# Neighbour lists split by upper and lower 64 rows in a four-layer graph attention kernel, and more row blocks worked on over all nodes

## The chip, the core and the metric

The kernel runs on one core of one Trainium2 chip, in one launch. The metric is device time in microseconds (us); lower is better. In the profile the engines are PE (TensorE matmuls), PEld (TensorE weight loads), DVE (VectorE), ACT (ScalarE), POOL (GpSimd) and SP (SyncE, which starts most DMAs).

## What is computed

There are 4096 nodes with 256 features and an adjacency matrix `adj` of 4096 x 4096 zeros and ones; a pair is an edge with a chance of 1/256, and the diagonal is set. Four attention layers follow one another, each with a residual and a layer norm: `x = layernorm(x + layer(x, adj))`.

```python
# layers 0 and 1: 4 heads of 64; layer 2: 2 heads of 128
e = leaky_relu(s[:, None] + d[None, :], 0.2)      # s, d: linear in x, per head
e = where(adj > 0, e, -inf)
out = softmax(e, axis=-1) @ h                      # h: a linear map of x, per head
# layer 3: one score, two softmaxes (of e and of -e), values of 256
new = concat([softmax(e) @ x, -softmax(-e) @ x]) @ fc_W;  out = elu(new)
```

## The kernel before

**Sparse row tiles.** The nodes are cut into 32 tiles of 128. For a row tile of 128 nodes, about 1600 of the 4096 nodes are neighbours of at least one of its rows. `Program.lists` (L293) finds them once, before and during layer 0. For each row tile it packs the neighbours into 13 list tiles of 128 places (`NG`), and adds the row tile itself as a 14th (`NP`). It does so with one-hots: `pack` (L427) compares, for each of the 31 other node tiles, the place of each node with a range of places (L440, on DVE), and multiplies the one-hot with the mask bytes on PE (L446). `windows` (L106) gives the range that a node tile's places can fall into, so that a one-hot is one to three list tiles wide. The result is `maskC`, the 128 x 14 x 128 mask bytes of a row tile, and `idx`, the node number of each place. `places` (L394) works the places out, per block of four row tiles. If a list overflows, a flag is set and a dense fallback runs after the packed program.

**Attention of one row tile** (`RowTile`, L606). It is done in two halves of seven list tiles. `load` (L632) starts the DMAs: the score row `S`, the mask, the row tile's own values, and an indirect gather on POOL for each of the other list tiles (L647), which brings 128 rows of `vals` (values and score terms of the layer, `ROW[n]` floats) into a buffer `G`. First-half gathers read only the first 17 node tiles (`MIX`), so that they can start before all of the layer's values are there. `half` (L651) then makes the weights `w`, 128 list nodes by 128 rows per list tile: three of the four heads in layers 0 and 1 with one ACT exponential per list tile (L712), the fourth with DVE products (L704, L708); then one DVE operation per pair of heads clamps and masks seven list tiles of both (L681). In layers 0 and 1 the matmul (L724) has the values as weights (65 columns) and moves the 128 columns of `w`, so the result is transposed, and `copy` and `back` (L744, L751) turn it again. In layers 2 and 3 the matmul (L727) has `w` as weights (128 columns) and moves the values (129 or 257 columns). The arithmetic is fp32; one such matmul is two instructions, each with its own weight load.

**Row blocks over all nodes.** `WHOLE` (L94) lists blocks of four row tiles that use no lists: blocks 3, 7 and 6 in layer 2, and 7 in layer 3. `whole_rows` (L982) goes over all 32 node tiles, with exponentials (L1016, L1019 to L1023), masks (L1017, L1024) and matmuls (L1027). It is a generator, and `whole` (L804) advances it between the halves of the sparse row tiles, so that its work is spread over the layer.

**Order.** `part` (L812) goes over the row tiles, half by half. In layers 0 and 1 `half_alone` (L827) also projects finished row tiles for the next layer (`Projection`, L531); in layers 2 and 3 `half_with_whole` (L859) does, and advances the whole blocks. `close` (L919) passes from one layer to the next. `norm` (L1049) gathers row tiles in groups (`GROUPS`, L76) for the inverse square root. Each engine's final order is set by a scheduler from priorities in program order.

The `G` buffers: `g0` has 16 slots of two list tiles (one in layer 3), `g1` 14.

Of the kernel before, what the change touches and what calls it, by code (L numbers as in the profile page):

```python
# [50 lines left out]
P = 128  # L51
N = 4096
F = 256
# [17 lines left out]
NG = 13  # L71
NP = NG + 1
CAP = NG * P
HALF = NP // 2

GROUPS = (((24, 4),), ((28, 2),), ((16, 2), (17, 1), (20, 2), (24, 1), (31, 2)), ((28, 1), (31, 4)))  # L76
LEAD = 10
MIX = 17
FRONT = 6
NODES = tuple(MIX * P if t < FRONT else N for t in range(NG))  # L80
MC = P + 4
# [6 lines left out]

LOGS = (3, 3, 2, 1)
# [3 lines left out]
KEXP = 10.0  # L93

# [4 lines left out]
WHOLE = ((), (), (3, 7, 6), (7,))  # L99
# [6 lines left out]
def windows():  # L106

    share = 1.0 - (1.0 - 1.0 / 256.0) ** P
    mean, sd = P * share, (P * share * (1.0 - share)) ** 0.5
    dev = 4.5  # L110
    out = {}
    for m in range(NT):
        for j in range(NT):
            if j == m:
                continue
            if j < MIX:
                n = sum(q != m for q in range(j))
                lo = mean * n - dev * sd * n ** 0.5
                hi = mean * (n + 1) + dev * sd * (n + 1) ** 0.5
            else:  # L120
                n = sum(q != m for q in range(j, NT))
                lo = CAP - mean * n - dev * sd * n ** 0.5
                hi = CAP - mean * (n - 1) + dev * sd * (n - 1) ** 0.5
            a = max(0, int(lo // P))
            b = min(NG - 1, int((hi - 1) // P))
            out[m, j] = (a, b - a + 1)
    return out
# [3 lines left out]
assert all(a >= FRONT for (m, j), (a, _) in WINDOW.items() if j >= MIX)  # L131
WMAX = max(n for _, n in WINDOW.values()) * P
# [7 lines left out]
def kernel(ctx: ExitStack, tc: tile.TileContext, ins: dict, out: bass.AP):  # L140
# [11 lines left out]
        "shift2": const.tile([P, 1], F32, name="shift2"),  # L152
        "shift3": const.tile([4, 4], F32, name="shift3"),
        "zero": const.tile([4, 4], F32, name="zero"),
        "maskC": dram.tile([NT, P, NP, MC], U8, name="maskC"),
# [8 lines left out]
    nc.vector.memset(shared["shift2"], -2.0 * KEXP)  # L164

# [28 lines left out]
class Program:  # L194


    def __init__(self, tc, ctx, ins, out, shared):
# [5 lines left out]
        self.g0 = self.pool("g0", 16)  # L203
# [6 lines left out]
        self.masks = None  # L210
# [82 lines left out]
    def lists(self, ctx):  # L293
# [21 lines left out]
        for k, sh in enumerate((8, 4, 0)):  # L315
# [21 lines left out]
        nc.gpsimd.affine_select(out=bt[:, :, :MIX], in_=bt[:, :, :MIX], pattern=[[NT, BT], [1, MIX]],  # L337
                                compare_op=ALU.is_gt, fill=0.0, base=0, channel_multiplier=-1)
        nc.vector.tensor_scalar(bt[:, :, MIX:], bt[:, :, MIX:], -1.0, None, op0=ALU.mult)

        nc.gpsimd.affine_select(out=bt[:, :, MIX:], in_=bt[:, :, MIX:], pattern=[[-NT, BT], [-1, NT - MIX]],
                                compare_op=ALU.is_ge, fill=0.0, base=-MIX, channel_multiplier=1)


        lo = cst.tile([P, NT, NT], F16, name="lo")
        wid = cst.tile([P, NT, NT], F16, name="wid")
        nc.gpsimd.memset(lo, 0.0)
        nc.gpsimd.memset(wid, 0.0)
        for j in range(NT):
            m = 0  # L350
            while m < NT:
                if m == j:
                    m += 1
                    continue
                e = m
                while e < NT and e != j and WINDOW[e, j] == WINDOW[m, j]:
                    e += 1
                a, n = WINDOW[m, j]
                nc.gpsimd.memset(lo[:, m:e, j], a * P - 1.0 - (CAP if j >= MIX else 0))
                nc.gpsimd.memset(wid[:, m:e, j], float(n * P))  # L360
                m = e
        limit = cst.tile([P, NP], F32, name="limit")
        nc.vector.memset(limit[:, :FRONT], float(MIX * P - 1))
        nc.vector.memset(limit[:, FRONT:], float(N - 1))
        total = cst.tile([P, NT], F32, name="total")
        bad = cst.tile([P, BT, NT], F32, name="bad")
        nc.vector.memset(bad, 0.0)

        class Block:
            def __init__(self, blk):  # L370
                self.blk = blk
                self.mk = mkp.tile([P, NT, BT, MC], U8, name="mk")
                self.red = wk.tile([P, BT, NT], F32, name="red")

            def prepare(self, part):
# [5 lines left out]
                for q in range(q0, q1, 2):  # L381
# [4 lines left out]
                nc.vector.tensor_copy(mkw[:, q0:q1, :, P // 4:],  # L386
                                      digw[:, q0:q1].rearrange("p (j t o) -> p j t o", t=1, o=1)
                                      .to_broadcast([P, JG, BT, 1]))
                nc.vector.tensor_reduce(self.red[:, :, q0:q1].rearrange("p t j -> p j t"),
                                        mkw[:, q0:q1, :, :P // 4], AX.X, ALU.max)  # L390
# [3 lines left out]
            def places(self):  # L394
                blk = self.blk
                if any(blk in w for w in WHOLE):
                    nc.sync.dma_start(out=shared["maskW"][blk], in_=self.mk)
                hit = wk.tile([P, BT, NT], BF16, name="hit")
                nc.vector.tensor_scalar(hit, self.red, 0.0, None, op0=ALU.is_gt)
                flat = hit.rearrange("p t j -> p (t j)")  # L400
                nc.vector.memset(flat[:, blk * BT:blk * BT + (BT - 1) * (NT + 1) + 1:NT + 1], 0.0)
                pt = prog.bank(prog.pthree)
                nc.tensor.matmul(pt[:, :P], flat, ones, start=True, stop=True)
                totals = wk.tile([P, P], BF16, name="totals")
                nc.scalar.copy(totals, pt[:, :P])
                pq = prog.bank(prog.pthree)
                nc.tensor.matmul(pq[:, :P], tri, flat, start=True, stop=False, skip_group_check=True)
                nc.tensor.matmul(pq[:, :P], totals, bt.rearrange("p t j -> p (t j)"), start=False, stop=False,
                                 skip_group_check=True)
                nc.tensor.matmul(pq[:, P:P + BT], totals, tot, start=False, stop=True, skip_group_check=True)  # L410
                ms = slice(blk * BT, (blk + 1) * BT)
                self.place = wk.tile([P, BT, NT], F32, name="place")
                here = self.place
                nc.vector.tensor_tensor(here, pq[:, :P].rearrange("p (t j) -> p t j", t=BT), lo[:, ms, :],
                                        op=ALU.subtract)
                nc.vector.tensor_tensor(here, here, hit, op=ALU.mult)
                nc.vector.tensor_copy(total[:, ms], pq[:, P:P + BT])

                for col in (wid[:, ms, :], None):
                    off = wk.tile([P, BT, NT], F32, name="off")  # L420
                    if col is None:
                        nc.vector.tensor_scalar(off, here, 0.0, None, op0=ALU.is_lt)
                    else:
                        nc.vector.tensor_tensor(off, here, col, op=ALU.is_gt)
                    nc.vector.tensor_tensor(bad, bad, off, op=ALU.max)
# [180 lines left out]
class RowTile:  # L606
# [144 lines left out]
    def back(self):  # L751
        L = self.layer
        if L.n >= 2:
            return
# [835 lines left out]
```

## Time and profile before

| | us |
|---|---|
| median of three runs | 2251.94 (2251.93 to 2260.22) |
| span of the profiled execution | 2249.3 |
| PE busy | 2014.0 (90%), 15689 instructions |
| DVE busy | 1786.6 (79%), 5060 |
| ACT busy | 1737.9 (77%), 4989 |
| POOL busy | 1494.4 (66%), 1597 |

The span runs from the first to the last instruction of one execution. The costliest groups of instructions are below (line, engine, operation, out<-in, partitions x elements, count; busy us, mean ns of one; idle time of the engine just before them and what ended it):

```profile
L647 POOL DMA_INDIRECT G<-vals,idx x1456 | 1480.7, 1017 | 715.7 <-issue 221.1
L712 ACT ACTIVATE w<-S,G 128x128 f32<-128x128 f32 x3248 | 1001.6, 390 | 140.6 <-DMA G<-vals,idx 101.6
L724 PE MATMUL bank<-w,G 128*65 128x128 f32 x7168 | 837.8, 276 | 59.7 <-DVE w L681 59.3
L681 DVE SCALAR_TENSOR_TENSOR w<-w,bank 128x1792 f32<-128x1792 f32 x256 | 514.6, 2013 | 13.4 <-ACT w L712 11.2
L727 PE MATMUL bank<-G,w 128*128 128x257 f32 (+1 forms) x2660 | 490.8, 342 | 25.7 <-ACT z L1102 13.6
L446 PE MATMUL bank<-mk,oh 128*128 128x132 fp8e4 x2336 | 192.1, 226 | 13.8 <-ACT cm L453 7.0
```

Busy time counts overlapping instructions of an engine once, so a group's busy time divided by its count is nearer to the pace than the mean of one.

### The profile page before, as it was taken

The numbers are of one execution on the slowest core, as the hardware profiler recorded it, in microseconds if no ns is written. First come the engines' busy times: TensorE is split into PE (matmuls) and PEld (weight loads), VectorE is DVE, ScalarE is ACT, GpSimd is POOL, SyncE is SP. The second block draws the span as 40 slices with busy tenths as digits, with TensorE's granted clock in tenths as the row PEclk, the third lists the DMA queues.
The fourth block names the chain that finished last, engine by engine and source line by source line (L and its number), as shares of the span: only waits on it lengthen the run. The fifth ranks groups of instructions, "written<-read, shape, count | busy, mean of one in ns | idle before, by whom it ended". The sixth has DMA issues, their size and how long they took to land. (4 is left out here: it accounts for less than half of the span.)

```text
span 2249.3 us, 49137 instructions
## 1 busy us (share of the span) xinstructions
PE 2014.0 (90%) x15689; PEld 1834.3 (82%) x15689; DVE 1786.6 (79%) x5060; ACT 1737.9 (77%) x4989; POOL 1494.4 (66%) x1597
## 2 busy tenths in 40 slices
PE   4878889989999969988899898989999999999995
PEld 2658788878899859988888798989998888788784
DVE  2889899999999959987988886887876566566566
ACT  4778988988789859987888776987876677667664
POOL 2107655656677777777777777777773477777773
PEclk7999999999999989999999999999999999999998
DMA  8879877777566665666665666777777688888884
GB/s 284 258 245 360 272 219 250 254 247 228 146 170 191 174 202 168 182 175 175 173 185 162 172 167 171 226 209 223 223 227 225 200 282 280 249 284 270 262 248 130
DMA packets 250319, 492.99 MB, mean 219 GB/s; under 512 B 44385, under 2 KB 156610, under 8 KB 249666
## 3 DMA queue, kind: packets, MB, share of 16 engines
q0 software_dynamic: 81536, 245.30, 38.3%
q1 hardware_dynamic: 163906, 240.26, 33.3%
q10 hardware_dynamic: 4608, 4.20, 0.5%
q8 instruction: 126, 2.06, 0.4%
q14 instruction: 143, 1.17, 0.2%
HBM read 437.05 MB, written 52.54 MB: 218 GB/s over the span
## 5 line engine op out<-in xcount | busy, mean ns | idle before, releaser
L647 POOL DMA_INDIRECT G<-vals,idx x1456 | 1480.7, 1017 | 715.7 <-issue 221.1
L712 ACT ACTIVATE w<-S,G 128x128 f32<-128x128 f32 x3248 | 1001.6, 390 | 140.6 <-DMA G<-vals,idx 101.6
L724 PE MATMUL bank<-w,G 128*65 128x128 f32 x7168 | 837.8, 276 | 59.7 <-DVE w L681 59.3
L724 PEld LDWEIGHTS bank<-w,G 128*65 128x65 f32 x7168 | 798.7, 140 | 69.9 <-DVE w L681 68.4
L681 DVE SCALAR_TENSOR_TENSOR w<-w,bank 128x1792 f32<-128x1792 f32 x256 | 514.6, 2013 | 13.4 <-ACT w L712 11.2
L727 PE MATMUL bank<-G,w 128*128 128x257 f32 (+1 forms) x2660 | 490.8, 342 | 25.7 <-ACT z L1102 13.6
L727 PEld LDWEIGHTS bank<-G,w 128*128 128x128 f32 x2660 | 431.9, 195 | 73.2 <-ACT z L1102 16.4
L1027 PE MATMUL bank<-vw,pw 128*128 128x129 f32 (+1 forms) x2048 | 298.5, 301 | 3.7 <-issue 2.3
L1027 PEld LDWEIGHTS bank<-vw,pw 128*128 128x128 f32 x2048 | 273.6, 191 | 20.1 <-issue 2.8
L690 ACT ACTIVATE w<-S,G 128x128 f32<-128x128 f32 x385 | 137.8, 393 | 136.8 <-DMA G<-vals,idx 90.0
L440 DVE TENSOR_SCALAR oh<-iota,place 128x256 bf16<-128x256 f16 (+2 forms) x992 | 221.8, 298 | 9.4 <-PE bank L446 9.1
L704 DVE TENSOR_TENSOR w<-S,G 128x256 f32<-128x256 f32 x384 | 151.9, 416 | 69.9 <-DMA G<-vals,idx 66.5
L446 PE MATMUL bank<-mk,oh 128*128 128x132 fp8e4 x2336 | 192.1, 226 | 13.8 <-ACT cm L453 7.0
L557 PE MATMUL bank<-wext,xT 128*128 128x268 f32 (+3 forms) x640 | 176.9, 409 | 16.9 <-ACT xT L548 14.1
L446 PEld LDWEIGHTS <-oh 128*128 128x128 bf16 x2336 | 146.9, 99 | 50.4 <-DVE oh L440 12.7
L385 ACT ACTIVATE mk<-raw 128x1024 uint8<-128x1024 int32 x128 | 130.5, 1051 | 28.0 <-DMA raw<-in_adjB_dram 27.7
L557 PEld LDWEIGHTS bank<-wext,xT 128*128 128x128 f32 x640 | 117.2, 200 | 36.0 <-ACT xT L548 16.9
L1017 DVE SCALAR_TENSOR_TENSOR pw<-pw,mw 128x512 f32<-128x512 f32 x192 | 127.6, 689 | 18.2 <-ACT pw L1016 17.5
L1016 ACT ACTIVATE pw<-Sw,d 128x512 f32<-128x512 f32 x192 | 133.2, 711 | 7.5 <-PE bank L1027 7.0
L714 DVE SCALAR_TENSOR_TENSOR w<-w,mk 128x896 f32<-128x896 f32 x80 | 86.6, 1086 | 41.1 <-ACT w L712 37.9
L1024 DVE TENSOR_TENSOR pw<-pw,mw 128x512 f32<-128x512 f32 x64 | 43.6, 691 | 85.4 <-ACT pw L1023 48.0
L692 DVE TENSOR_TENSOR w<-w,mk 128x896 f32<-128x896 f32 x55 | 60.0, 1091 | 59.5 <-ACT w L691 58.2
(140 smaller groups left out, 1563.3 us busy)
## 6 DMA issues: line engine op xcount, KB each, us to landing
raw<-in_adjB_dram SPq DMA_DIRECT2D x128, 512.0 KB
mk<-maskC SPq DMA_DIRECT2D x112, 231.0 KB
G<-vals,idx POOLq DMA_INDIRECT x1456
S<-edge SPq DMA_DIRECT2D x64, 256.0 KB
vw<-vals SPq DMA_DIRECT2D x96, 129.0 KB
xp<-y SPq DMA_DIRECT2D x96, 128.0 KB
y<-xp SPq DMA_DIRECT2D x96, 128.0 KB
mw<-maskW SPq DMA_DIRECT2D x20, 528.0 KB
```

What stands on the lines that cost most here:

```text
L440: nc.vector.tensor_scalar(oh[:, :n * P], iota[:, :n * P], self.place[:, it, j:j + 1], None, op0=ALU.is_equal)
L446: nc.tensor.matmul(accs[b][:, s * MC:(s + 1) * MC], oh[:, (k - a) * P:(k - a + 1) * P], mk[:, j, it, :].bitcast(FP8), start=touches[b][0] ...
L557: nc.tensor.matmul(pp[:, :c1 - c0], self.xT[:, k, :], wext[:, k, c0:c1], start=(k == 0), stop=(k == KT - 1 and brow is None))
L647: nc.gpsimd.indirect_dma_start(out=self.place(pos), out_offset=None, in_=sh["v"][n][:NODES[t], :], in_offset=bass.IndirectOffsetOnAxis(ap= ...
L681: nc.vector.scalar_tensor_tensor(pair, pair, LEAST, mh2, op0=ALU.max, op1=ALU.mult)
L690: nc.scalar.activation(w[0][:, k, :], S[:, 0, :], AF.Relu, bias=d(k, 0))
L704: nc.vector.tensor_tensor(w[h][:, k:k + 2, :], S[:, h:h + 1, :].to_broadcast([P, 2, P]), dd[:, :, V + T + h:V + T + h + 1].to_broadcast([P ...
L712: nc.scalar.activation(w[h][:, k, :], S[:, h, :], AF.Exp, bias=d(k, h))
L724: nc.tensor.matmul(accs[0][:Wd, h * P:(h + 1) * P], v, w[h][:, k, :], **how)
L727: nc.tensor.matmul(a, w[h][:, k, :], v, **how)
L1016: nc.scalar.activation(p, S[:, h], AF.Exp, bias=d)
L1027: nc.tensor.matmul(accs[it][:, c:c + Wd], p[:, it, :], v[:, c:c + Wd], start=(j == 0 and h == heads[0]), stop=(j == NT - 1), skip_group_ch ...
```

## The change

1. **Lists.** A neighbour of a row tile is put into one of three classes: it is adjacent to rows 0 to 63 only, to rows 64 to 127 only, or to both. Five list tiles hold the first class, five the second, three the third and what overflows from the first two. There are 13 gathers per row tile as before, but an upper and a lower tile share one 128 x 128 unit of weights, 64 columns each: 9 units per row tile (five pairs, three whole, the row tile's own) instead of 14. `maskC` is 9 units wide. The first half has the row tile itself and three pairs (four units), the second two pairs and three whole list tiles (five).
2. **Weights and matmuls.** A pair's exponentials are done in two instructions of 64 columns, with each list tile's own bias. In all layers `w` is now the matmul's weights and the values are moved. A list tile of a pair has 64 weight columns and writes output rows 0 to 63 or 64 to 127, so a pair is two matmuls. `copy` and `back` are gone. Within a half, pairs and whole units are kept together.
3. **Whole blocks.** `WHOLE` has blocks 7 and 6 in layer 1 and 7 and 6 in layer 3. A new generator, `whole_heads`, does layer 1's: the weights are a product of a row term and a node term, so one DVE operation per head and node tile makes, clamps and masks them, without ACT. Two heads are worked on together, one with the weights `p` loaded, the other with the values loaded and turned afterwards.
4. **Buffers and limits.** `g0` and `g1` have four slots, each of seven list tiles (four in layer 3). First-half gathers read the first 23 node tiles. The groups of `norm` are fitted to the new order.

The core of the diff (`places` is longer by the arithmetic of the classes):

```diff
-NG = 13
-NP = NG + 1
-HALF = NP // 2
+NPAIR = 5
+NMIX = 3
+NPACK = NPAIR + NMIX
+NU = NPACK + 1
+NP = 2 * NPAIR + NMIX
+HALF = 7
+FIRST = 3
+UNITS = (1 + FIRST, NPACK - FIRST)
+FULL = ((0,), tuple(range(NPAIR - FIRST, NPACK - FIRST)))
+PAIRS = (tuple(range(1, 1 + FIRST)), tuple(range(NPAIR - FIRST)))
-MIX = 17
+MIX = 23
+TWOS = ((3, 0), (2, 1))
-WHOLE = ((), (), (3, 7, 6), (7,))
+WHOLE = ((), (7, 6), (3, 7, 6), (7, 6))
-        self.g0 = self.pool("g0", 16)
+        self.g0 = self.pool("g0", 4)
-        self.g1 = self.pool("g1", 14)
+        self.g1 = self.pool("g1", 4)
...
             def pack(self, it):
...
+                def parts(j):
+                    a, n, e, x = WINDOW[j]
+                    return list(range(a, a + n)) + list(range(NPAIR + e, NPAIR + e + x))
...
-                    nc.vector.tensor_scalar(oh[:, :n * P], iota[:, :n * P], self.place[:, it, j:j + 1], None,
-                                            op0=ALU.is_equal)
-                    for k in range(a, a + n):
+                    nc.vector.tensor_scalar(oh[:, :len(ks) * P], iota[:, :len(ks) * P], self.place[:, it, j:j + 1],
+                                            None, op0=ALU.is_equal)
+                    for i, k in enumerate(ks):
...
             for h in range(A):
-                for k in range(HALF):
-                    nc.scalar.activation(w[h][:, k, :], S[:, h, :], AF.Exp, bias=d(k, h))
+                for u in range(U):
+                    for rows, g in parts[u]:
+                        nc.scalar.activation(w[h][:, u, rows], S[:, h, rows], AF.Exp, bias=d(g, h))
...
-                if n < 2:
-                    nc.tensor.matmul(accs[0][:Wd, h * P:(h + 1) * P], v, w[h][:, k, :], **how)
-                else:
-                    a = accs[h][:, :Wd] if n == 3 else accs[0][:, h * Wd:(h + 1) * Wd]
-                    nc.tensor.matmul(a, w[h][:, k, :], v, **how)
+        for t, heads in enumerate(turns):
+            for us in (FULL[half], PAIRS[half])[::-1 if t == 1 and (half == 1 or n < 3) else 1]:
+                for h in heads:
+                    for u in us:
+                        for rows, g in parts[u]:
+                            a = accs[h][rows, :Wd] if n == 3 else accs[0][rows, h * Wd:(h + 1) * Wd]
+                            nc.tensor.matmul(a, w[h][:, u, rows], g[:, h * Wd:(h + 1) * Wd],
+                                             start=half == 0 and u == 0 and (n == 3 or h == turns[0][0]),
+                                             stop=half == 1, skip_group_check=True)
...
+    def whole_heads(self):
...
+        c = prog.bk.tile([P, NT, T], F32, name="cw")
+        nc.scalar.activation(c, sh["d"][n], AF.Exp, bias=sh["shift1"])
...
+                    for h in (up, flat):
+                        p[h] = prog.dp.tile([P, BT, P], F32, name="pw")
+                        nc.vector.scalar_tensor_tensor(p[h], S[:, h], c[:, j, h:h + 1], mj, op0=ALU.max, op1=ALU.mult)
+                    how = dict(stop=j == NT - 1, skip_group_check=True)
+                    for it in range(BT):
+                        nc.tensor.matmul(bu[:, it * Wd:(it + 1) * Wd], p[up][:, it, :],
+                                         v[:, up * Wd:(up + 1) * Wd], start=j == 0 and it == 0, **how)
+                        nc.tensor.matmul(bf[:Wd, it * P:(it + 1) * P], v[:, flat * Wd:(flat + 1) * Wd],
+                                         p[flat][:, it, :], start=j == 0 and it == 0, **how)
+                    yield
```

## The prediction

> **What bounds the kernel now.** I read the profile stage by stage, because the page's shares (PE 90%, DVE 79%, ACT 77%, POOL 66%) average over stages with different limits. The stage borders come from first and last starts: the lists' one-hots (L440) run from 56.8 to 641.0 us, ten lists before layer 0's first attention and 22 beside it; layer 0 ends at 812, layer 1 at 1346, layer 2 at 1742, and the last matmul of layer 3 starts at 2226. The view of windows over these borders (columns: window; busy us and instructions of PE, PEld, DVE, ACT, POOL; granted clock; DMA share; GB/s):
>
> ```profile
> 57.00:165.00 108.00, 90.54 (x893) 69.82 (x893) 94.57 (x423) 80.69 (x205) 7.69 (x8) 0.94 0.80 251
> 165.00:644.00 479.00, 428.80 (x4282) 392.87 (x4283) 461.96 (x1374) 414.50 (x1232) 305.96 (x301) 0.98 0.75 244
> 644.00:812.00 168.00, 156.42 (x1351) 149.89 (x1350) 154.35 (x378) 146.61 (x509) 126.44 (x131) 0.99 0.65 181
> 812.00:1346.00 534.00, 474.81 (x3995) 443.89 (x3993) 445.47 (x1011) 437.33 (x1470) 406.44 (x419) 0.97 0.63 175
> 1346.00:1742.00 396.00, 371.52 (x2977) 357.57 (x2977) 303.94 (x855) 308.25 (x839) 284.10 (x259) 0.98 0.75 215
> 1742.00:2226.00 484.00, 461.76 (x2083) 399.01 (x2083) 299.60 (x909) 321.93 (x682) 350.10 (x342) 0.98 0.82 255
> ```
>
> POOL looks slack until its timeline is read: a gather is busy 0.95 us, and 0.30 us pass before the next although nothing is waited for.
>
> ```profile
> 924.65 0.94 POOL L647 DMA_INDIRECT G<-vals,idx  x1 [0.30 <-issue]
> 925.90 0.95 POOL L647 DMA_INDIRECT G<-vals,idx  x1 [0.30 <-PE bank L724]
> 927.15 0.94 POOL L647 DMA_INDIRECT G<-vals,idx  x1 [0.30 <-issue]
> ```
>
> So POOL is full at one gather per 1.255 us, 16.3 us per row tile of 13. Layer 1's 419 gathers need 526 of its 534 us: POOL bounds it. The tail of layer 0 too (131, 164 of 168). In 165 to 644 it is DVE, 462 of 479 us. Layer 2 has two near limits (PE 372; POOL 284 busy and 259 x 0.30 = 362, of 396). Layer 3 is bound by PE (462 of 484), with POOL behind it (342 x 1.255 = 429). The chain of waits, in layer 3, is nothing but matmuls (start, us, what):
>
> ```profile
> 1846.88 1.73 PE bank L1027 x8
> 1848.61 6.07 PE bank L727 x28
> 1854.68 1.73 PE bank L1027 x8
> ```
>
> **PE rows to price with.** An fp32 matmul is two instructions, each with its weight load.
>
> ```profile
> 820.19 0.95 PE L278 MATMUL bank<-ablk,nat 128*128 128x2 f32 x8
> 821.24 1.05 PE L278 MATMUL bank<-ablk,nat 128*128 128x2 f32 x8
> 905.48 6.28 PE L724 MATMUL bank<-w,G 128*65 128x128 f32 x56
> 911.60 0.27 PE L589 MATMUL bank<-ident,row 128*2 128x128 f32 x1
> 911.71 0.38 PE L543 MATMUL bank<-ident,y 128*128 128x128 f32 x2
> 1848.45 6.23 PE L727 MATMUL bank<-G,w 128*128 128x257 f32 x28
> ```
>
> 257 moving columns cost 0.217 each (6.07/28). 128 columns under a 65-column load: (6.28-0.28)/55 = 0.109. L278 moves only 2 columns, so its (1.05-0.25)/7 = 0.114 is the price of loading 128 weight columns; I use 0.112. So an instruction costs the larger of 0.00085 us per moving column and 0.00088 us per weight column.
>
> **The change, part by part.**
>
> *Lists, DVE.* One-hots stay 992, mean width 262 columns to 488 (341 of 640, 248 of 512, 279 of 384, 124 of 256). By the groups 256 cost 0.291 and 384 cost 0.316, 0.02 per 100, so 640 is 0.383: mean 0.299 to 0.345, +1.42 us per list. The placing grows from nine operations per block (2.1 us) to 13 of 256 elements (0.416 each, the row of L704), 9 of 128 (0.286, L414) and some small ones: 10.3 us, +8.2 per block, +2.05 per list. Small ones +0.25. Together +3.7 per list. PE: 2336 to 3782 packing matmuls at 0.07 (57 in 4.13 us at L446), +3.2 per list.
>
> *Sparse attention, layers 0 and 1, DVE.* A row tile has 9 units instead of 14 tiles of weights. Mask: 4 x 2.013 becomes 2 x 1.22 and 2 x 1.48 (1.035 ns per element, from 896 = 1.086 and 1792 = 2.013), -2.65. Products: 6 x 0.416 + 2 x 0.295 becomes 2 x 0.551 + 0.416 + 0.295, -1.27. Mask copy -0.17. In all -4.1, to 7.8 us per tile (5.4 + 1.8 + 0.6).
>
> *PE there.* Out go 112 instructions of 0.109 (12.2 us) and the transposes back (4 in 0.46). In come 80 with 64 weight and 65 moving columns and 32 with 128 and 65. The 32 are bound by their load, 0.112. For the 80 no row exists: at most 0.109 (L724), at least 0.025 (four tiny ones of L287 in 0.24, less their latency); by columns 0.058, which I take. 80 x 0.058 + 32 x 0.112 = 8.2, -4.3 us per tile. ACT: 42 exponentials (0.29 apart) become 30 of 64 columns and 12 of 128, about -1.6 us, never first.
>
> *Layer 0's sum.* From 57 to 165 (ten lists, no attention, DVE at 88%, PE at 84%): DVE +3.7 x 10 = +37, of which slack takes some 12: **+25 us**. From 165 to 644: 22 x (3.7-4.1) = **-9**. Its tail is POOL's, 13 gathers as before: 0. Range -5 to +60, the end being both engines' growth in a row.
>
> *Layer 1.* 8 of 32 tiles leave POOL: 24 x 16.3 = 392 us against 526. But they go to PE and DVE. PE: sparse 24 x 8.2 = 197; dense 2048 instructions, half with 128 weight and 65 moving columns, half the reverse, alternating in pairs so that a long load lies under a long matmul: two long, one short and one long in four, (3 x 0.112 + 0.058)/4 = 0.098, 200 us; the rest as before, 475 - 3584 x 0.109 - 8 = 76; 96 switches between whole-array and half-array weights. Bounds for a switch: nothing (L589, with 2 weight columns, lies between L724 and L543 without a gap) and 0.09 (L560, one weight row, is 0.98 behind four L557 that take 0.88). I take 0.09: 9 us. Sum 482. DVE: 445 - 32 x 4.1 - 8 x 7.8 + 256 x 0.67 (L1017) + 6 = 428. PE is the new bound; at the 97% that DVE reached in layer 0, 497 of 534: **-37**. Range -75 (POOL and PE even at 455) to 0.
>
> *Layer 2.* Its tiles need 20 x 56 instructions of 0.112 now, then 20 x (40 x 0.058 + 16 x 0.112), -43 on PE if two halves run beside each other in the array, nothing if not. POOL stays at 362: **-12**, range -25 to +5.
>
> *Layer 3.* POOL: 24 tiles instead of 28. Only two tiles' first halves now fit in the slots ahead, not four, so about 303 gathers fall into the stage, 380 us. PE: dense 1024 x 0.217 = 222 instead of 111; a sparse tile has 16 whole instructions (3.5 us) and 40 with 64 weight columns and 257 moving ones. These cost 0.217 if alone in the array, 0.109 if the upper and the lower half stream side by side. No row shows two at once. I take side by side, because the halves write different output partitions, hold different weights and are emitted alternately: 24 x (3.5+4.4) = 188; sum 188 + 222 + 11 (rest) + 11 (120 switches) = 432, and 22 us of gaps as before, 454 of 484: **-30**. The other end is worked out below.
>
> *Costed at nothing.* A slot now holds seven gathers (four in layer 3), so a gather waits for the last matmul of a whole half, and all later gathers queue behind it on POOL. Four slots per pool leave POOL three halves ahead, 3 x 8.2 = 24 us, and a half needs some 15 us (6.5 of exponentials, 2 x 1.4 of masks, 4 of matmuls). Should that cover go, POOL idles up to 4 us per half, 190 us over layer 1. First halves now read 23 node tiles, not 17; at both layer ends these are projected before the last tile, and the second half waits for all 32 as before. SP issues 192 more loads of some 130 KB, POOL 156 fewer gathers of as much; DMA is busy 63% in layer 1 and 82% in layer 3, so they hide.
>
> [...] With a full latency of a matmul (0.27) at each of some 500 switches the sum would lose another 90 us.
>
> Sum: 25 - 9 - 37 - 12 - 30 = -63. The profiled execution spans 2249.3 us; 2186 after. The median of the runs shown, 2251.94, lies 2.6 above the span: **2189 us**.
>
> **Rivals.**
> 1. *The halves don't run side by side (slower).* Place: layer 3's PE. Price: 40 x 0.108 x 24 = 104 us more, 536 + 22 = 558 of 484, +74; layer 2 gains 0; layers 0 and 1 keep theirs, since 65 moving columns are short. 25 - 9 - 37 + 0 + 74 = +53: 2305. It decides once a half costs over 0.17 instead of 0.109. For it: PE already bounds this stage and gets a whole dense block more. Against: distinct output rows.
> 2. *The lists and DVE take the gain back.* Phase 57 to 165 pays +50, from 165 on the longer placing chain (PE, ACT, PE, then 22 dependent DVE operations) stalls the full DVE, +15, and layer 1, with DVE at 428 and PE at 482 feeding each other, reaches 88%: 548, +14. 50 + 15 + 14 - 12 - 30 = +37 at its worst, and +5 in the middle: 2257.
> 3. *POOL remains the only bound.* Switches cost nothing, PE needs 470 in layer 1 and runs without gaps, layer 3 follows POOL with 380 + 40: 15 - 9 - 60 - 20 - 55 = -129: 2123.
>
> **Chances.** The sum as worked 0.50 (2150 to 2235), rival 1 0.21, rival 2 0.15, rival 3 0.14. Faster or slower than 0.5% (11 us, about what a measurement can tell): the sum 0.48 faster; rival 3 all; rival 2 0.05 faster, 0.06 same, 0.04 slower; rival 1 slower. Faster 0.67, same 0.08, slower 0.25. The range takes in most of rivals 1 and 3: 2115 to 2305; the likeliest case alone is 2150 to 2235.
>
> **What would show it.** Side by side: pairs of the 64x257 row 0.11 apart on average, not 0.217. Layer 1: about 500 us, PE over 95% busy, POOL with waits. Lists: the last one-hot later than 641 by 10 to 30 us. Layer 0's tail still one gather per 1.255 us. Layer 3 near 455 us. I am wrong if layer 3 grows, or if a switch leaves gaps of 0.2 us on PE.

## The result, and the profile after

The changed kernel takes 2319.51 us (median of four runs, 2312.40 to 2335.76) where before takes 2256.08 beside it (2251.93 to 2260.27): ratio 1.0294, 95% interval 1.0265 to 1.0323. It is **slower**; the forecast was 2189. The profiled execution took 2323.15 us, its span is 2321.4.

The stages, by the prediction's borders (first one-hot, L504; end of the tenth and of the last list; statistics of a layer's last row tile; start of the last matmul):

| stage | before | after | forecast | measured |
|---|---|---|---|---|
| to the first one-hot | 57 | 70 | with the next | +13 |
| ten lists | 108 | 153 | +25 | +45 |
| 22 lists beside attention | 479 | 531 | -9 | +52 |
| tail of layer 0 | 168 | 173 | 0 | +5 |
| layer 1 | 534 | 513 | -37 | -21 |
| layer 2 | 396 | 395 | -12 | -1 |
| layer 3 | 484 | 468 | -30 | -16 |
| end | 23 | 18 | | -5 |
| sum | 2249 | 2321 | -63 | +72 |

The same windows in after's trace (columns as in the prediction):

```profile
70.00:223.00 153.00, 120.19 (x1408) 102.40 (x1409) 125.49 (x495) 81.01 (x194) 16.71 (x12) 0.87 0.67 216
223.00:754.00 531.00, 438.18 (x5130) 401.65 (x5126) 455.26 (x1453) 338.67 (x1115) 285.10 (x293) 0.75 0.63 193
754.00:927.00 173.00, 136.17 (x1336) 117.81 (x1337) 118.42 (x360) 128.32 (x509) 126.29 (x132) 0.74 0.66 186
927.00:1440.00 513.00, 469.98 (x5015) 424.55 (x5011) 433.56 (x1045) 292.51 (x1112) 303.60 (x293) 0.92 0.65 187
1440.00:1835.00 395.00, 357.69 (x3014) 327.10 (x3015) 284.43 (x868) 294.03 (x852) 272.50 (x260) 0.96 0.71 204
1835.00:2303.00 468.00, 447.33 (x2386) 328.39 (x2384) 278.82 (x890) 328.22 (x744) 319.08 (x312) 0.98 0.84 268
```

The second row is the surprise. DVE is busy 455 us, where the forecast had 462 - 9 = 453, yet the stage is 531 long. DVE fills 86% of it (before 96%), PE 83%, and PE's granted clock is 0.75 where it was 0.98. Layers 2 and 3 kept their clock (0.96 and 0.98, before 0.98 in both). The page's slices show it over the whole span: it is 6 to 8 tenths up to the 17th slice (986 us), and 9 after that but for one slice within layer 1 and the ends of layers.

```profile
PE   4867787888788868699899989797999899989996
PEld 2757787777677757699788986787989767757774
DVE  2978988888888767699897986477787746565665
ACT  4554757676655867546545665587788568766873
POOL 0012654455446677777746630777777177767773
PEclk7878777777778786799989997899999999999998
```

POOL's pace is unchanged, 1.25 us from one gather to the next (tail of layer 0, timeline):

```profile
821.95 0.95 POOL L714 DMA_INDIRECT G<-vals,idx  x1 [0.30 <-PE bank L819]
823.20 0.95 POOL L714 DMA_INDIRECT G<-vals,idx  x1 [0.30 <-issue]
824.45 0.95 POOL L714 DMA_INDIRECT G<-vals,idx  x1 [0.30 <-issue]
```

**How the clock falls.** Six neighbouring windows of 3.4 us in after, within the 22 lists (columns as above; the granted clock stands behind the five engines):

```profile
303.30:306.70 3.40, 3.33 (x57) 3.15 (x54) 3.40 (x11) 1.11 (x2) 2.49 (x4) 1.00 0.98 385
306.70:310.10 3.40, 1.01 (x9) 1.01 (x10) 3.39 (x11) 3.40 (x13) 2.49 (x4) 1.00 1.01 318
310.10:313.50 3.40, 2.52 (x27) 2.00 (x28) 3.05 (x9) 3.40 (x15) 0.96 (x1) 0.51 1.00 375
313.50:316.90 3.40, 3.40 (x28) 3.28 (x27) 2.79 (x9) 3.40 (x15) 0.00 (x0) 0.50 0.58 216
316.90:320.30 3.40, 3.40 (x38) 3.16 (x38) 0.58 (x2) 1.81 (x7) 2.25 (x3) 0.50 0.16 40
320.30:323.70 3.40, 3.40 (x63) 3.19 (x61) 3.36 (x9) 0.00 (x0) 2.48 (x4) 0.99 0.47 126
```

In the second window PE works 1.01 of 3.4 us, because it waits 2.46 us for the masks of the next half (L763). The following three windows run at half clock: 27 to 38 matmuls instead of 57 to 63. PE is full from the second of them on, and in the fifth window DVE does 0.58 us of work, since its one-hot buffers wait for PE. So each engine waits for the other in turn. Counted over the whole span from the trace's clock records, the clock was halved 52 times in after and 23 times in before.

Half of the 531 us, 268, run at half clock. DVE is busy in 93% of the time at full clock and in 79% of that at half clock, and of the 55 us that it waits for one-hot buffers here, 44 fall at half clock. The same wait in before, in its stage of 479 us (us, times, longest):

```profile
DVE oh L440 <- PE bank L446: 4.3, 1, 4.3
```

### The profile page after: what moved, and what is told of

It reads as the page before. It is cut to its first block, busy times and chain, and to the rows that moved or that the text cites. A ratio compares the mean times of both kernels' runs of the same rounds, so it can differ in the third digit from the quotient of the medians.

```text
span 2321.4 us, 54044 instructions
## 1 busy us (share of the span) xinstructions
PE 2002.1 (86%) x18383; PEld 1723.4 (74%) x18383; DVE 1730.0 (75%) x5248; ACT 1499.3 (65%) x4596; POOL 1328.9 (57%) x1374
## 5 line engine op out<-in xcount | busy, mean ns | idle before, releaser
L714 POOL DMA_INDIRECT G<-vals,idx x1300 | 1323.3, 1018 | 955.4 <-issue 380.7
L819 PE MATMUL bank<-G,w 128*64 128x65 f32 (+5 forms) x8708 | 844.7, 299 | 119.4 <-DVE w L763 100.2
L819 PEld LDWEIGHTS bank<-G,w 128*64 128x64 f32 (+1 forms) x8708 | 694.2, 180 | 272.0 <-DVE w L763 114.7
L805 ACT ACTIVATE w<-S,G 128x64 f32<-128x64 f32 (+1 forms) x2912 | 784.3, 352 | 129.9 <-DMA G<-vals,idx 107.6
L1102 PE MATMUL bank<-vw,pw 128*128 128x129 f32 (+1 forms) x2560 | 422.8, 323 | 18.0 <-issue 6.7
L1102 PEld LDWEIGHTS bank<-vw,pw 128*128 128x128 f32 x2560 | 377.4, 196 | 58.8 <-issue 18.1
L763 DVE SCALAR_TENSOR_TENSOR w<-w,bank 128x1024 f32<-128x1024 f32 (+1 forms) x224 | 301.3, 1346 | 34.8 <-ACT w L805 34.1
L504 DVE TENSOR_SCALAR oh<-iota,place 128x640 bf16<-128x640 f16 (+3 forms) x992 | 284.3, 351 | 57.2 <-PE bank L510 56.7
L510 PE MATMUL bank<-mk,oh 128*128 128x136 fp8e4 x3782 | 263.2, 232 | 6.3 <-ACT cm L516 4.0
L510 PEld LDWEIGHTS <-oh 128*128 128x128 bf16 x3782 | 248.3, 103 | 13.5 <-DVE oh L504 4.5
L1162 DVE SCALAR_TENSOR_TENSOR pw<-Sw,cw,mw 128x512 f32<-128x512 f32 x256 | 183.6, 740 | 1.4 <-issue 1.2
L1165 PE MATMUL bank<-vw,pw 128*128 128x65 f32 x1024 | 151.7, 267 | 17.8 <-DVE pw L1162 17.8
L1167 PE MATMUL bank<-pw,vw 128*65 128x128 f32 x1024 | 163.3, 277 | 0.0
L773 ACT ACTIVATE w<-S,G 128x64 f32<-128x64 f32 (+1 forms) x329 | 104.6, 352 | 85.4 <-DMA G<-vals,idx 47.7
L1165 PEld LDWEIGHTS bank<-vw,pw 128*128 128x128 f32 x1024 | 139.9, 195 | 20.9 <-issue 19.6
```

The costliest lines, as they stand in the source:

```text
L504: nc.vector.tensor_scalar(oh[:, :len(ks) * P], iota[:, :len(ks) * P], self.place[:, it, j:j + 1], None, op0=ALU.is_equal)
L510: nc.tensor.matmul(accs[b][:, s * MC:(s + 1) * MC], oh[:, i * P:(i + 1) * P], mk[:, j, it, :].bitcast(FP8), start=touches[b][0] == (j, k), ...
L714: nc.gpsimd.indirect_dma_start(out=self.place(half, k), out_offset=None, in_=sh["v"][n][:N if half else MIX * P, :], in_offset=bass.Indire ...
L763: nc.vector.scalar_tensor_tensor(pair, pair, LEAST, mh2, op0=ALU.max, op1=ALU.mult)
L805: nc.scalar.activation(w[h][:, u, rows], S[:, h, rows], AF.Exp, bias=d(g, h))
L819: nc.tensor.matmul(a, w[h][:, u, rows], g[:, h * Wd:(h + 1) * Wd], start=half == 0 and u == 0 and (n == 3 or h == turns[0][0]), stop=half ...
```

## The experiments

Two kinds of chips were met. On those of the result above and of e1 to e4, before takes 2254 to 2256 us. On three others before takes 2752 to 2798 and after 2868 to 2920, ratio 1.0385 to 1.0474. There the stages ahead of the attention are as long as ever (after's ten lists take 153 to 155 us), the later ones longer. Kernels are compared on their own kind of chip. In the table, layers end with the statistics of their last tile, also layer 3; rounded us:

| kernel | before there | total | ratio, 95% interval | first one-hot | ten lists | 22 lists | layer 1 | layer 2 | layer 3 |
|---|---|---|---|---|---|---|---|---|---|
| before | | 2256.1 | | 57 | 109 | 478 | 534 | 396 | 495 |
| after | 2256.1 | 2319.5 | 1.0294 (1.0265-1.0323) | 70 | 154 | 531 | 514 | 394 | 479 |
| e1 | 2253.8 | 2335.1 | 1.0349 (1.0290-1.0407) | 70 | 153 | 520 | 527 | 383 | 505 |
| e2 | 2253.8 | 2300.5 | 1.0199 (1.0153-1.0244) | 69 | 154 | 509 | 524 | 382 | 480 |
| e3 | 2253.8 | 2284.3 | 1.0161 (1.0107-1.0214) | 69 | 180 | 471 | 514 | 392 | 479 |
| e4 | 2253.8 | 2296.1 | 1.0185 (1.0144-1.0226) | 71 | 150 | 507 | 515 | 396 | 478 |
| e5 | 2797.6 | 2891.1 | 1.0328 (1.0282-1.0373) | 69 | 153 | 724 | 705 | 506 | 521 |
| e6 | 2797.6 | 2915.9 | 1.0412 (1.0361-1.0463) | 62 | 145 | 737 | 712 | 505 | 522 |
| e7 | 2797.6 | 2927.0 | 1.0460 (1.0421-1.0499) | 70 | 153 | 750 | 718 | 485 | 517 |
| e8 | 2797.6 | 2941.2 | 1.0498 (1.0459-1.0537) | 69 | 153 | 752 | 701 | 514 | 522 |
| a1 (after) | 2789.3 | 2919.9 | 1.0474 (1.0435-1.0514) | 68 | 155 | 746 | 686 | 508 | 515 |
| e9 (= e5) | 2789.3 | 2903.6 | 1.0382 (1.0309-1.0455) | 68 | 153 | 723 | 710 | 503 | 518 |
| e10 | 2789.3 | 2851.5 | 1.0222 (1.0182-1.0262) | 60 | 121 | 712 | 703 | 502 | 517 |
| e11 | 2789.3 | 2902.4 | 1.0390 (1.0343-1.0437) | 70 | 170 | 698 | 729 | 492 | 520 |
| a2 (after) | 2755.1 | 2868.1 | 1.0385 (1.0336-1.0434) | 70 | 153 | 740 | 675 | 507 | 511 |
| e12 (= e5) | 2755.1 | 2830.8 | 1.0292 (1.0243-1.0342) | 69 | 153 | 705 | 651 | 507 | 511 |
| e13 | 2755.1 | 2843.4 | 1.0309 (1.0265-1.0353) | 61 | 152 | 720 | 675 | 496 | 513 |
| e14 | 2755.1 | 2797.1 | 1.0155 (1.0120-1.0189) | 62 | 153 | 722 | 675 | 447 | 511 |
| e15 (= e5) | 2751.7 | 2834.9 | 1.0277 (1.0187-1.0367) | 68 | 156 | 711 | 662 | 506 | 513 |
| e16 (= e14) | 2751.7 | 2802.3 | 1.0168 (1.0110-1.0225) | 62 | 172 | 698 | 676 | 464 | 513 |

The border between the two list stages shifts from one profile to another: e14 and e16 are the same kernel on the same chip, and have 153 and 722 us against 172 and 698. The sum of the two is steadier (875 and 869).

My theory after the result: in layer 0, PE's shorter work leaves it waiting, its clock is halved, and then DVE waits for it (theory A). The rival: the lists' own work on DVE and PE sets the stage (theory C).

### The clock in layer 0: e3, e4, e5 and its repeats

e3 adds products that nobody reads, only to keep PE moving:

```diff
                         nc.tensor.matmul(accs[b][:, s * MC:(s + 1) * MC], oh[:, i * P:(i + 1) * P], ...)
+                        if i == 0 and j % 2 == 0 and touches[b][-1] != (j, k):
+                            nc.tensor.matmul(accs[b][:, 3 * MC:3 * MC + 104], shared["ident"],
+                                             shared["ident"][:, :104], start=False, stop=False, ...)
```

> After with one more product of the identity (fp32, 104 columns, into unused columns of the bank) behind every other one-hot of a list, 14 a list: work whose result nobody reads, to keep TensorE from standing still. Theory A (layer 0's stages are long because TensorE's clock is halved after windows in which it waits for one-hots, and DVE then waits for it): the granted clock of 223 to 754 us rises from 0.75 to over 0.9 and the stage falls by 30 us or more, to a total of 2290 or less. Theory C (the work of the lists on DVE and TensorE sets the stage): the clock may rise, but the stage gets longer by up to the added 448 x 0.2 = 90 us.

Its two list stages in the view of windows:

```profile
69.00:249.00 180.00, 154.50 (x1683) 142.09 (x1682) 137.27 (x523) 86.30 (x209) 17.86 (x19) 0.90 0.60 195
249.00:721.00 472.00, 437.62 (x5808) 412.12 (x5807) 448.79 (x1436) 335.07 (x1111) 286.56 (x287) 0.92 0.68 215
```

The 22 lists fall from 531 to 472 us at a clock of 0.92, with 678 more matmuls on PE, and with DVE, ACT and POOL about as busy as in after (449, 335 and 287 us against 455, 339 and 285). So hardly any work was shifted out of the stage (some 6 us of DVE's); with more matmuls it is shorter. DVE's wait for one-hot buffers in that stage, us, times and longest, is first after's (223 to 754 us), then e3's (249 to 721 us):

```profile
DVE oh L504 <- PE bank L510: 55.2, 42, 2.5
```

```profile
DVE oh L504 <- PE bank L510: 15.6, 20, 2.3
```

All of theory A's forecasts were met; theory C's, a longer stage, was not. The lists' work counts here as well, though: in e10, with narrower lists, this stage is 34 us shorter than in a1 on the same chip (712 against 746) at a still lower clock, 0.64 against 0.70 (0.786 against 0.801 over the whole span). Against my expectation the ten lists grew by 26 us, where PE's busy time grew by 34 (120 to 154): there most of its work counts. The total is 35 us under after.

One rival stays open. The products also change the order that the scheduler gives: up to the last list, 66% of PE's sequence and 57% of DVE's agree with after's (in a2, the same kernel as after, all). In e1 and e2, which leave this stage's work as it is, 70% of PE's and 93% of DVE's agree, and the stage moves by 11 and 22 us, with the clock: 531, 520, 509 and, in e3, 471 us go with 0.75, 0.76, 0.80 and 0.93. That speaks for the clock, and the 59 us of e3 are beyond that spread; no run changes the clock and keeps the order.

e4 gives DVE more one-hot buffers, `pool("oh", 16)` for `pool("oh", 8)`.

> After with 16 buffers of one-hots in place of 8. Theory A (DVE waits about 57 us for TensorE to free one-hots, as TensorE's order puts them behind attention products): DVE's waits on one-hots fall by half or more, TensorE finds more of them ready, the clock rises, and the time falls by 15 to 40 us to 2280 to 2305. Theory C: the time stays within 5 us of 2319.

Its total is 23 us under after, and DVE's wait for buffers falls from 52 to 17.5 us (both between 223 and 720 us). Both are as forecast. But the 22 lists, 507 us at a clock of 0.79, are hardly below e2's 509 and e1's 520, whose work differs from after's there by one copy of 0.15 us per projected tile. So the buffers' part is not told apart from the stage's own spread of some 20 us; e3's 472 lies outside it.

e5 adds the products from the eleventh list on (`m >= 10 and` in e3's condition).

> The added identity products of e3_warm only in the 22 lists that are made beside attention (row tiles 10 to 31); the ten lists before are as in after. Theory A (clock): the ten lists take after's 153 us instead of the 180 of e3_warm, the 22 lists the 472 of e3_warm instead of 531, so the total is 2250 to 2268, level with before: the whole loss to before is then the clock's. If e3_warm's gain came from lists that its slower start had put ahead, the 22 lists take 490 us or more and the total stays over 2280.

> The kernel of e5_warm_late once more, beside after itself. Theory A (clock): against after on the same chip the 22 lists beside attention are 40 us or more shorter, everything ahead of them the same, the total lower by 40 to 65. If the halved clock is only a mark of a TensorE that waits and costs nothing, within 10 us of after.

> The kernel of e5_warm_late on a third chip, for a chip on which before takes about 2254. Theory A (clock): the ten lists as in after (153 us), the 22 lists 472 instead of 531, the total 2255 to 2275 and 45 to 65 below after. If e3_warm's gain was only a shift of work into its longer first stage, 490 or more and over 2285.

> The kernel of e12 once more. On a chip where before takes about 2254: by theory A (clock) the ten lists 153 us, the 22 lists 465 to 485, the total 2255 to 2275 (ratio to before 1.000 to 1.010); otherwise over 2285. On a chip where before takes 2750 to 2800 it says no more than before: 15 to 40 us under after.

All four met the slower chips, so the number that mattered (about 2260) was not tested. What they show is the sign: beside after on the same chip the 22 lists are 23 us (e9, 746 to 723) and 35 us (e12, 740 to 705) shorter with nothing lengthened ahead, and the clock is higher (e9: 0.826 over the whole span against 0.801 in a1; e12: 0.80 in this stage against 0.70 in a2). The 40 us forecast for e9 were not reached. The totals fall by 16 and 37 us, in e9 with runs that overlap with after's. The stage in a2, and below it in e12:

```profile
222.00:962.00 740.00, 538.29 (x5130) 471.80 (x5126) 472.00 (x1455) 338.55 (x1116) 279.26 (x293) 0.70 0.46 140
```

```profile
222.00:927.00 705.00, 548.88 (x5788) 492.10 (x5785) 465.83 (x1459) 340.55 (x1125) 282.36 (x293) 0.80 0.49 146
```

### The lists: e6, e10, e13

e6 deletes the twelve operations that test for overflow (seven on `move`, five on `back`).

> After without the twelve DVE operations per block that test whether a list overflows (7 of 256 elements, 5 of 128; the fallback on overflow is left out). By their rows that is 7 x 0.416 + 5 x 0.286 = 4.3 us of DVE per block, behind each other before the block's first one-hot. Theory P (the first one-hot's +13 us and the ten lists' +45 come from the longer placing chain): first one-hot 4 us earlier, the ten lists 9 to 13 us shorter. Theory W (they come from the one-hots and packing products, wider and more): start 4 us earlier, the ten lists no more than 5 us shorter. From 223 us on, where DVE has slack in after, no more than 10 us by either.

The first one-hot comes at 62 us, 69 or 70 in the other kernels on that chip, and the ten lists take 144 to 145 instead of 153:

```profile
62.00:207.00 145.00, 118.13 (x1390) 102.10 (x1391) 121.88 (x480) 81.22 (x203) 16.70 (x14) 0.90 0.72 230
```

The twelve operations cost 7 us at the start, more than the 4.3 of their busy time: in after's timeline DVE puts other work between them (rows of projections, the next block's reductions) and waits 1.7 us. Over the ten lists they cost 9, about the busy time of the two blocks that come there.

e10 sets also `dev = 0.2` for `dev = 4.5` in `windows`.

> After without the overflow tests (as e6) and with one-hots only as wide as the mean place of a node tile's entries: 2387 packing products instead of 3782 and one-hots of 308 columns on average instead of 488 (before: 2336 and 262). Entries that fall outside are left out of the lists, so that part of the attention is missing. Theory W (the ten lists are long by their wider one-hots and more packing products, 3.2 us of TensorE and 1.4 of DVE per list): from after's 153 us they fall by 30 to 40 us, 9 of it by the tests left out. Theory P (by the placing chain): by 9 to 15.

```profile
60.00:181.00 121.00, 95.39 (x924) 74.93 (x922) 104.83 (x473) 79.36 (x197) 7.86 (x8) 0.89 0.76 244
```

Ten lists in 121 us, 32 less than after's 153 and in theory W's range: 9 by the tests and 23 by narrower one-hots and 1395 fewer packing products. So both theories have their share. Of the 58 us that the change lost by the end of the tenth list, the tests are 16, and width and number of the one-hots 25 (2 of it before the first one-hot). The other 17 were not divided further; the rest of the placing is in them, and what e10's one-hots are still wider than before's (308 columns against 262).

e13 moves the twelve tests behind the block's second list (on top of e5's products).

> e12 with the twelve overflow tests of a block moved from ahead of its first one-hot to behind its second list: the same DVE work off the chain that the first one-hot waits for. Theory P (the first one-hot is late by the longer chain): first one-hot 7 us earlier than in e12, the ten lists 3 to 9 shorter, the total 8 to 16 below e12. If DVE's work counts and not the chain: first one-hot earlier, the ten lists longer by as much, the total within 5 of e12.

The first one-hot comes 8 us earlier than in e12, and the ten lists are about as long (152 against 153), so nearly 10 us are won by their end: the chain counts. In the total nothing is left of the 8 to 16 forecast: 2843.4 (2831.7 to 2850.8) against 2830.8 (2822.3 to 2849.1). Whether the 22 lists gave it back or it is scatter of that chip is open.

### The whole blocks: e1, e2, e7, e14 and e16

e1 takes before's `WHOLE` and fitting `GROUPS`, so it is the pairs alone; e2 takes away layer 1's blocks alone:

```diff
-WHOLE = ((), (7, 6), (3, 7, 6), (7, 6))
+WHOLE = ((), (), (3, 7, 6), (7,))      # e1
+WHOLE = ((), (), (3, 7, 6), (7, 6))    # e2
```

> The kernel after with before's whole blocks (layer 1 none, layer 3 one): the pairs and their lists alone. Theory A (layer 0 carries the loss, and layer 1's two blocks give back at the change to layer 2 what they save): layer 0 as in after (its first sparse tile of layer 1 at about 922 us), layer 1 with 32 sparse tiles some 525 to 540 us with no long gap of POOL behind it, layer 3 about 475 to 485, so 2320 to 2345 us in all, close to after. Theory B (the two blocks cost the time, the lists do not): below 2270.

> After without the two whole blocks of layer 1; layer 3 keeps both of its own. Theory A: layers 1 and its change to layer 2 take 525 to 540 us together, as the 528 of after, so the time is 2310 to 2335 us and POOL has no gap over 40 us between layers 1 and 2. If the blocks' steady saving of 534 - 444 = 90 us were real and only the gap of 84 us were an accident of something else (the pairs' wider first halves), the gap would stay and the time would be about 2400.

Layers 1 and 2 of e2:

```profile
902.00:1426.00 524.00, 411.60 (x3869) 346.30 (x3867) 334.28 (x879) 371.65 (x1439) 398.07 (x414) 0.70 0.61 171
1426.00:1808.00 382.00, 346.87 (x3002) 318.62 (x3001) 284.58 (x860) 292.05 (x846) 266.17 (x246) 0.96 0.72 206
```

With 32 sparse tiles layer 1 is POOL's (416 gathers x 1.25 = 520 of 524 us) and ten us longer than in after; layer 2 is 12 shorter. 906 us against 908: layer 1's two blocks bring nothing. POOL suggests why. After's waits (us, times, longest) have one of 88.9 us, from 1361.5 to 1450.4 us, and e2 has none between these layers. The view puts its end down to L1102, layer 2's dense matmuls, but names only what ended last; rows of `vals`, which the gathers read, are still being stored up to 1445 us.

```profile
POOL G L714 <- PE bank L1102: 95.6, 23, 88.9
...
POOL G L714 <- PE bank L819: 42.9, 32, 9.2
```

Layer 2's first halves read 23 node tiles, and with the order 0 to 23 the last of these is normalised when layer 1 ends; before read 17 of 32. Layer 3's second block is worth e1 - e2: 505 to 480, 25 us. e1's total lies in the range forecast, e2's 10 us below its own. e2's total is 19 us under after, where the 22 lists alone are 22 shorter; whether that is the stage's spread is open.

e7 spreads the dense units over `2 * count + 8` instead of `2 * count - 6` steps in layer 1.

> After with layer 1's dense units spread over 56 instead of 42 steps, so that some 18 of 128 are left behind the last sparse tile. Theory G (layer 2's gathers stand still for 88 us because the node tiles that its first halves read are finished last, while TensorE is busy with dense work): they start some 40 us or more before layer 1 ends, layers 1 and 2 together fall from 908 to 885 to 900 us, the total by 8 to 23. Rival (TensorE's work of layer 1 sets both): within 5 us of after.

POOL's gap ends 53 us before layer 1 does, as forecast, where in after and all kernels with after's steps it ends 7 to 10 us behind it. But it is hardly shorter (83 us, against 84 to 100 in e8, e6 and e5 on that chip), and layers 1 and 2 together take 1203 us against 1210 to 1217 there: the sign as expected, the size within the scatter. In e11, with the same steps, the gap ends 61 us before layer 1 does and the two layers are no shorter. So the late gathers are not shown to be what the blocks' saving is lost by.

e14 is e13 with e2's edit.

> e13 without layer 1's two whole blocks. Theory G (the blocks' saving in layer 1 is lost again because layer 2's gathers then start late): layer 1 10 us longer, layer 2 12 shorter, the total within 6 us of e13, as e2 beside after in these two layers. If e2's 19 us less than after came from these layers, 15 or more below e13. Either way a little below before, 2230 to 2250 where before takes 2254.

> The kernel of e14 once more. On a chip where before takes about 2254: first one-hot at 62 us, the 22 lists 465 to 485, layers 1 and 2 together 900 to 910, the total 2240 to 2262, level with before. If layer 1's blocks are worth their steady saving after all, 20 or more above the kernel beside it.

Layer 1 is as long as with blocks (675), layer 2 takes 447 us instead of 496, POOL's gap of 89 us between them is gone, and the total falls by 46 us; it falls by 33 between e15 and e16, which differ by e13's move of the tests as well. Theory G had 6 at most, so its size falls on these chips: there layer 1's blocks cost time. No kernel here beat before: e3 at 1.016 and e14 at 1.0155 come nearest.

### Side by side: e8

e8 emits a group's upper halves ahead of its lower ones.

> After with the upper halves of a group of pairs all ahead of its lower halves, in all layers: the same instructions, but consecutive ones share their output rows. If side by side is what the pairs live on, a 64x257 instruction costs 0.217 us instead of 0.128: layer 3 longer by 24 x 40 x 0.09 = 86 us, layer 2 by 20 x 40 x 0.06 = 48 less its slack of some 15, layers 0 and 1 by 0 to 30 (65 columns), in all 2420 to 2470. If the saving came from the fewer weight columns alone, within 15 us of after.

The edit did not do what it was for. In the trace twelve 64x257 instructions in a row (six upper, six lower) take 1.935 us from the first to the instruction behind them, 0.161 each, where after's take 1.451, 0.121 each: PE still started lower halves beside upper ones. Layer 3 in e8 and in e6 on the same chip:

```profile
2411.00:2923.00 512.00, 478.79 (x2354) 353.91 (x2354) 281.63 (x895) 333.13 (x747) 319.73 (x312) 0.96 0.79 245
```

```profile
2383.00:2894.00 511.00, 460.83 (x2345) 332.62 (x2344) 280.86 (x891) 331.15 (x744) 318.35 (x312) 0.94 0.79 245
```

18 us more of PE, and the stage is as long. That halves run side by side is therefore shown by the trace alone: in after the second of a pair starts 6 to 7 ns behind the first, the next pair 210 ns later, so that two take the time of one whole instruction (217 ns). e11, which joins e5, e4 and e7, and a1, after itself:

> After with e5's identity products, e4's 16 buffers of one-hots and e7's later dense units. If the three act on separate things: the 22 lists beside attention 465 to 475 us, layers 1 and 2 together 8 to 15 shorter than in after on the same chip, the total 2240 to 2260 where before takes 2254. If the clock is all that the buffers gave, no shorter than e9 by more than 15.

> The kernel after, unchanged, as the reference of the runs beside it and to see how much its stages vary from one profile to another: its 22 lists beside attention within 505 to 535 us, every other stage within 4 us of the first profile (70, 153, 173, 513, 395, 468).

Against a1, e11's 22 lists are 48 us shorter, the ten lists 15 longer and layers 1 and 2 together 27 longer, in all 17.5 less: the gains do not add up. a1's and a2's stages and totals were not as expected, since their chips are of the slower kind.

## Why the prediction was wrong, step by step

- **"From 165 to 644: 22 x (3.7-4.1) = -9" failed: +52.** The DVE sum was right to 2 us (453, measured 455). What failed is the step from busy time to stage: it took for granted that DVE stays full at 96%; DVE filled 86%. PE got lighter (at full clock its work would take some 330 us against 420 before, an estimate from its busy time at either clock), stood 93 us instead of 50, ran at half clock for half of the stage, and then held up DVE (55.2 us of waits for one-hot buffers, 4.3 before). e3 makes this likely rather than certain, as its order is another too. Neither the sum nor a rival had the clock.
- **"Of which slack takes some 12: +25 us" failed: +58.** DVE grew by 31 us and PE by 30, near the 37 and 32 worked out. But the slack took none of it, and the 13 us before the first one-hot, which the longer placing costs first of all, stood in no term. The end of the range, "both engines' growth in a row" at +60 for layer 0, was all but reached by this stage alone.
- **Layer 1, "482 at the 97% that DVE reached": -21, not -37.** PE's work is 470 us, better than the sum; the share is 92%. PE is full from 975 to 1150 and from 1200 to 1370 us; of its 43 idle us, 20 come before, 14 between and 9 behind, and its two longest waits, 17.8 and 12.7 us, are ahead of the first dense block and between the two (us, times, longest):

```profile
PE bank L1165 <- DVE pw L1162: 17.8, 1, 17.8
PE bank L616 <- DVE y L1225: 15.2, 2, 12.7
```

  The sum had no term for them.
- **"At both layer ends these are projected before the last tile", costed at nothing, failed.** POOL stands 89 us; layer 2 loses 12 us, its whole forecast gain, which e2 shows without the blocks (396 to 382). That the loss comes by the gathers' late start is argued, not shown.
- **Layer 3: -16, not -30.** PE measured 447 busy and 21 idle against 432 and 22. The groups of that stage (busy us behind the bar):

```profile
L1102 PE MATMUL bank<-vw,pw 128*128 128x257 f32 x1019 | 234.6, 385 | 10.2 <-issue 5.8 <-DVE mv L1195 1.5 <-DVE rec L1258 1.4
L819 PE MATMUL bank<-G,w 128*64 128x257 f32 x944 | 120.6, 394 | 0.0
L819 PE MATMUL bank<-G,w 128*128 128x257 f32 x372 | 103.4, 402 | 8.8 <-DVE w L775 8.8
```

  Dense instructions cost 234.6/1019 = 0.230 against 0.217, halves 120.6/944 = 0.128 against 0.109, a sparse tile's whole ones 103.4/372 = 0.278 against 0.217; the switches lie in these figures. The mechanism is right and the size off.
- **Right:** halves side by side, which no row of before showed and after's trace shows (the second of a pair 6 to 7 ns behind the first), so rival 1 falls. A 64x65 instruction costs 225.9/4480 = 0.050 against the 0.058 taken, over both clocks; in rows of 24 it is 0.035 at full clock and 0.062 at half, so these halves run side by side too. POOL's 1.25 us and the tail of layer 0 (+5) held, and so did the coarser slots: POOL waited for L819 42.9 us in the whole span.
- **A switch, "I take 0.09", was too small.** At full clock it makes 0.093 us from start to start (205 against 112 ns), and the instructions behind come later by another 0.05 to 0.10 (101 against 52 ns, 321 against 217): 0.14 to 0.20 in all. The full latency of a matmul per switch (0.27), which was weighed, did not come.
- **Rivals:** the sign was rival 2's (0.15), with its +50 in the first phase measured as 58. Where it put +15 of stalls, the stage grew by 52, and hardly by the placing chain: e3 leaves that chain as it is and the 22 lists lose 59 us.

## What to carry to other kernels

Lightening PE where it shares a stage with the bound can lengthen the stage: here it waited in bursts, its granted clock was 0.75 where it had been 0.98, DVE waited 55.2 us for it where it had waited 4.3, and the stage took 531 us instead of 479. That the clock is the cause is likely by e3 (0.92 and 472 us), not certain; it belongs among the terms of the sum. Operations on the chain ahead of a stage's first instruction can cost more than their busy time (7 us against 4.3 in e6), since other work comes between them, and belong in the sum before any slack is counted. When row tiles leave the sparse order, ask which tile the next layer's first transfer needs, and when that one is done.

## What the runs showed of the hardware

**How the granted clock fell and rose in after.** The trace's clock records have two values, full clock and half, and last a multiple of 3.41 us, but for the one in which the program ends. Taken as windows of that length, and sorted by the share of the window in which PE was busy, they show this: of 36 windows at full clock with PE busy under 40%, all 36 were followed by half clock; of 40 between 40 and 70%, 16 were; of 427 over 70%, none. From half clock it rose 51 times, 50 of them after a window over 90% busy, and 43 times it stayed halved after such a window. Of the 52 falls, 36 came without a gap of PE as long as a window, by shorter gaps within one.

**PE stood between instructions on three chips.** On each of the three slower chips PE has long waits for nothing that the profile shows, before L819 164.2 us in a1, 161.1 in a2 and 187.2 in e7. a1's (us, times, longest):

```profile
PE bank L819 <- issue: 164.2, 250, 4.2
...
PE bank L1102 <- issue: 68.2, 58, 3.1
PE bank L510 <- issue: 56.8, 93, 1.2
```

and after's on the chip of the result, where the same view has no such wait at L819 and L510:

```profile
PE bank L1102 <- issue: 6.7, 2, 5.8
```

In 1200 to 1800 us of a1 these waits are 27.7 us at L819 (49 times, 1.2 at most) and 25.4 at L1167 (32 times, 2.5 at most). The cause was not found. Layer 1's blocks, worth nothing on the first kind of chip, cost 46 us on one of these (e13 against e14); whether by these waits was not tested.
